# Turned activations with the channel chunk innermost, layer norms turned through HBM, and maxima gathered off TensorE

## The chip, the core and the metric

The program runs on one core of a Trainium2 chip. The metric is device time in microseconds. Three runs of the kernel before took 1811.73 (the median), 1814.87 and 1811.0 us. Everything is float32. The engines are TensorE (PE in the profile; PEld is its weight load), VectorE (DVE), ScalarE (ACT), GpSimd (POOL) and SyncE (SP), which issues all DMAs in one queue. SBUF is the working memory of 128 partitions, PSUM the memory that TensorE writes to.

## What is computed

Two layers on X of shape (2, 1024, 512). Each layer normalises its input and adds to it causal attention with 16 heads of 32 channels (with rotary embedding) and a gated feed-forward, both fed with the same normalised input:

```python
xn = _layernorm(x, axis=-1)
x = x + _L0_attn_ref(xn, Wq, Wk, Wv, Wo) + _L0_ffn_ref(xn, w_gate, w_up, w_down)
xn = _layernorm(x, axis=-1)
x = x + _L1_attn_ref(xn, Wq, Wk, Wv, Wo) + _L1_ffn_ref(xn, gate_w, up_w, down_w, gate_s, up_s, down_s)
# attention: softmax(mask(rope(xn Wq.T) @ rope(xn Wk.T).T * 32 ** -0.5)) @ (xn Wv.T), then @ Wo.T
# feed-forward: (silu(xn gate.T) * (xn up.T)) @ down.T, hidden width 2048 in layer 0, 1408 in layer 1
```

## The kernel before

The work is four phases, one for each layer and batch entry: (layer 0, b 0), (0, 1), (1, 0), (1, 1). A phase has 1024 tokens in eight tiles x of 128, and the normalised input turned to channels by tokens in two halves xnT of 512 tokens. The 512 channels are four chunks of 128, so a half of xnT is a tile of 128 partitions by [4 chunks, 512 tokens], and one chunk's 512 tokens lie side by side in each partition.

Products of xnT go through a scheme with seven block products in place of eight (`Unit`, L710): one unit for each 128 hidden columns (`Hidden`, L1131: gate and up together), one for each group of four heads (`QueriesKeys`, L901), two for the values (`Values`, L951). A unit has four pieces. `first` multiplies with the first half of xnT, `second` with the differences xs, `third` with the second half, `fourth` with the last difference again. Every block product is two matmuls (`product`, L760), with the weights as the stationary operand and xnT or xs as the moving one, 512 columns; in `Values.product` (L992) it is the other way round, xnT or xs being loaded as the weights, 128 columns at a time. GpSimd makes xs from xnT (`ln_sums`, L680) and at last writes differences over the first two chunks of xnT's second half (`ln_last_sum`, L691).

Attention of a phase goes over four groups of four heads and, in each, four blocks of 256 queries, a `Run` (L1207): 64 runs of one to four steps, 160 steps in all. A step makes scores (sc), which ScalarE copies to SBUF with the factor (s). VectorE takes maxima of s over blocks of 32 keys and 32 queries (rmax), and at the end of a run over the keys (m1, `blocks`, L1259). `maxima` (L1278) then gathers the partitions' parts: TensorE turns m1 into a PSUM tile (mtr), VectorE reduces it to m2, SP writes m2 to HBM (md), and `spread` (L1288) reads it back to all 128 partitions (mb). `transpose_maxima` (L1199) holds a finished run until its m1 is there by the planner's times. VectorE then subtracts mb, ScalarE takes exponentials, GpSimd adds them up (acc), and four steps later TensorE multiplies them with the values (av).

Layer norm of the first phase is done at the start, in pairs of tiles (`ln_pair`, `transpose_pair`, L633). For later phases, tiles are loaded and their statistics taken some 22 steps before the phase ends (`load_raw`, `ln_stats`, `ln_factors`). At the end of the phase they are loaded a second time (xr), scaled by ScalarE in place (`ln_scale`, L661), turned by four TensorE transposes into a bank of PSUM (`ln_transpose`, L668, the tile tr) and copied to xnT by ScalarE. A phase's input was written to HBM a phase earlier, or is the program's.

Order comes from a planner. `Schedule` (L155) records every operation with an estimated cost and places it in time, so that nearly all operations have line 278 in the profile; `again` (L358) makes the final order for every engine from due times reckoned backwards from TensorE's. `queue_phase` (L1552) lists the work that fills the gaps of attention, and `Fill.choose` (L1503) picks from it. The tiles tr, mtr, ux, uy, uz, d and ps_o share three banks of PSUM. The pool `tmp` holds two tiles for each tag, among them "swapped" (also used for the rotary embedding) and "xs" (also xr); `xp`, with xnT, has one for each tag.

Of the kernel before, what the change touches and what calls it, by code (L numbers as in the profile page):

```python
# [18 lines left out]
P = 128  # L19
# [11 lines left out]
NSQ = QB // SQ  # L31
EPS = 1e-5
# [122 lines left out]
class Schedule:  # L155
# [31 lines left out]
    def cost(self, eng, method, args, kwargs, outs, ins):  # L187

        n = self.columns(outs[0]) if outs else 0
        if eng is self.sync:  # L190

            size = 4 * int(np.prod((outs or ins)[0].shape, dtype=int))
            return 450.0, 1900.0 + size / self.RATE
        if eng is self.tensor:
            if method == "transpose":
                mode, t = "full", 131.0
            else:
                lhs, rhs = args[1], args[2]
                small_k, small_m = lhs.shape[0] < P, lhs.shape[1] < P
                mode = "rows" if small_k else "columns" if small_m else "full"  # L200
                t = max(self.columns(rhs), 64) * 1.676 / (1 if mode == "full" else 4)
            if mode != self.mode:
                t += {"full": 218.0, "columns": 100.0, "rows": 200.0}[mode]
                self.mode = mode
            return t, t + 163.0
        m = max([n] + [self.columns(i) for i in ins])
        if eng is self.vector:
            if method == "stream_shuffle":
                t = 735.0
            elif method == "reciprocal":  # L210
                t = 204.0
            elif method == "tensor_reduce" and not kwargs.get("apply_transpose"):
                t = (150.0 if ins[0].tile.pool.psum else 110.0) + m * (0.93 if ins[0].tile.pool.psum else 1.85)
            elif method == "bn_aggr":
                t = 182.0
            else:
                t = 160.0 + m * 1.04
        elif eng is self.scalar:
            t = (190.0 if method == "activation" and args[2] in self.TABLES else 150.0) + 0.85 * n
            for k in ("bias", "scale"):  # L220
                t += 105.0 if isinstance(kwargs.get(k), View) else 0.0
            t += 140.0 if method == "mul" else 0.0
        elif method == "affine_select":
# [282 lines left out]
def two_layers(ctx: ExitStack, tc: tile.TileContext, x_in, attn_w, ffn_w, ffn_s, rope, out):  # L506
# [126 lines left out]
    def transpose_pair(pair):  # L633

        tb, h = divmod(pair, 2)
        if h == 0:
            xnT[0, tb] = xp.tile([P, DC, TB], F32, tag=f"xnT{tb}", name=f"xnT0_{tb}")
        xn = normed.pop((0, pair))
        for n in range(2):
            tr = p_st.tile([P, 2, DC, P], F32, tag="st", name=f"tr0_{2 * pair + n}")  # L640
            for c in range(DC):
                nc.tensor.transpose(tr[:, 0, c, :], xn[:, n, ts(c, P)], ident)
            (nc.vector.tensor_copy if n else nc.scalar.copy)(xnT[0, tb][:, :, ts(2 * h + n, P)], tr[:, 0])
        if tb == 1:
            for n in range(2):
                ln_sums(0, 2 * h + n)
# [14 lines left out]
    def ln_scale(ph, t):  # L661
        tb, q = divmod(t, 4)
# [3 lines left out]
        normed[ph, t] = s  # L666

    def ln_transpose(ph, t):  # L668
        tb, q = divmod(t, 4)
        if q == 0:  # L670
            xnT[ph, tb] = xp.tile([P, DC, TB], F32, tag=f"xnT{tb}", name=f"xnT{ph}_{tb}")
        s = normed.pop((ph, t))
        tr = bank(f"tr{ph}_{t}", (P, DC, P))
        for c in range(DC):
            nc.tensor.transpose(tr[:, c, :], s[:, ts(c, P)], ident)
        nc.scalar.copy(xnT[ph, tb][:, :, ts(q, P)], tr)
        if tb == 1:
            ln_sums(ph, q)

    def ln_sums(ph, q):  # L680

        if q == 0:
            xs[ph] = [xp.tile([P, 2, TB], F32, tag=f"xs{n}", name=f"xs{n}_{ph}") for n in (1, 2, 4)]
        t1, t2, t4 = (t[:, :, ts(q, P)] for t in xs[ph])
        b11, b21 = (xnT[ph, 0][:, 2 * c : 2 * c + 2, ts(q, P)] for c in range(2))
        b12, b22 = (xnT[ph, 1][:, 2 * c : 2 * c + 2, ts(q, P)] for c in range(2))
# [4 lines left out]
    def ln_last_sum(ph):  # L691

        for c in range(2):
            b12, b22 = xnT[ph, 1][:, c, :], xnT[ph, 1][:, 2 + c, :]
# [15 lines left out]
    class Unit:  # L710
# [49 lines left out]
        def product(self, bank, a, b, start=False):  # L760
            for c in range(2):
# [3 lines left out]
                    b[:, c, :],  # L765
# [14 lines left out]
        def needs(self, kind):  # L780

            if kind == "second":
# [7 lines left out]
        def first(self):  # L790
# [4 lines left out]
            self.product(self.x, a11, x0[:, 0:2], start=True)  # L795
            one = self.one = keep(self.x, f"p1{self.name}")
            z = bank(f"uz{self.name}")
            self.product(z, a12, x0[:, 2:4], start=True)
# [18 lines left out]
        def third(self, nxt):  # L817
            (_, _, s3, _), _, s4 = self.blocks()
            x1 = xnT[self.ph, 1]
            self.product(self.x, s3, x1[:, 0:2])  # L820
# [3 lines left out]
            self.product(self.y, s4, x1[:, 2:4])  # L824
# [59 lines left out]
    def project_qk(which, tokens):  # L884
# [4 lines left out]
        for c in range(DC):  # L889
            nc.tensor.matmul(  # L890
                ps, wqk[0, 0, which][:, c, :], xnT[0, half][:, c, at : at + n], start=(c == 0), stop=(c == DC - 1)
# [59 lines left out]
    class Values(Unit):  # L951
# [154 lines left out]
    def hidden(ph, k, tb):  # L1106
# [3 lines left out]
        def product(name):  # L1110
            ps[name] = bank(f"{name}{ph}_{k}_{tb}")
            for c in range(DC):
                nc.tensor.matmul(
                    ps[name], wgu[ph, k, name][:, c, :], xnT[ph, tb][:, c, :], start=(c == 0), stop=(c == DC - 1)
# [80 lines left out]
    found = []  # L1195

    def transpose_maxima(now=False):
        while found and (now or nc.settled(found[0].m1) <= nc.tensor.free):
            found.pop(0).maxima()  # L1199
            spread_maxima()  # L1200

# [5 lines left out]
    class Run:  # L1207
# [208 lines left out]
    class Fill:  # L1416
# [111 lines left out]
        def run(self, step, share, between=()):  # L1528

            spent = 0.0  # L1530
            while True:
# [5 lines left out]
                transpose_maxima()  # L1537
# [14 lines left out]
    def queue_phase(ph):  # L1552
# [48 lines left out]
        def raw(t):  # L1601
            if t < QC:
                load_raw(nxt, t)

        def scale(t):
            if t < QC:
                ln_scale(nxt, t)


        fill.main.insert(len(fill.main) - 2, (0.0, lambda: (raw(0), raw(1)), "other", None, 0))  # L1610
        fill.main.insert(len(fill.main) - 1, (0.0, lambda: scale(0), "other", None, 0))
        for t in range(QC):

            def one(t=t):
                ln_transpose(nxt, t)
                raw(t + 2)
                scale(t + 1)

            fill.add(0.7, one, "other", lambda t=t: [normed[nxt, t]])
            if t == 1:  # L1620
                fill.add(0.0, waits)
        fill.add(0.0, lambda: (ln_last_sum(nxt), marks.append(nxt)))
# [56 lines left out]
    for i in range(total + LAG):  # L1679
# [52 lines left out]
        transpose_maxima(True)  # L1732
        if run and n == run.steps - 1:
            found.append(run)
# [78 lines left out]
```

## Time and profile before

| | |
|---|---|
| runs | 1811.73 us median (1811.0 to 1814.87) |
| the profiled execution's own time | 1814.8 us |
| its span in the profile | 1812.9 us |
| granted clock of TensorE | 0.998 |
| instructions in the span | 25807 |
| DMA | 165.15 MB, mean 91 GB/s |
| chain that ended last | PE 89%, POOL 5%, DVE 3%, issue 1%, ACT 1%, DMA 1% |

The page gives each engine's busy time, a picture of the span in 40 slices, the chain of work that ended last, groups of instructions and DMAs. A group's line reads: line, engine, operation, out<-in by the program's names, shapes, count | busy us in total, mean ns of one | idle time before them, and what ended it. A line of waits gives engine, tile and line, whom it waited for, us in total, times, the longest. A line of the timeline gives the start, the length, the engine, the operation and how many were merged. Matmuls overlap and their ends are modelled, so the distance between two starts says more than a mean length does. Names that stand for several tiles are merged: m is both m1 and m2, ws the weight sums, s the scores.

### The profile page before, as it was taken

The numbers are of one execution on the slowest core, as the hardware profiler recorded it, in microseconds if no ns is written. First come the engines' busy times: TensorE is split into PE (matmuls) and PEld (weight loads), VectorE is DVE, ScalarE is ACT, GpSimd is POOL, SyncE is SP. The second block draws the span as 40 slices with busy tenths as digits, with TensorE's granted clock in tenths as the row PEclk, the third lists the DMA queues.
The fourth block names the chain that finished last, engine by engine and source line by source line (L and its number), as shares of the span: only waits on it lengthen the run. The fifth ranks groups of instructions, "written<-read, shape, count | busy, mean of one in ns | idle before, by whom it ended". The sixth has DMA issues, their size and how long they took to land.

```text
span 1812.9 us, 25807 instructions
## 1 busy us (share of the span) xinstructions
PE 1798.0 (99%) x9406; PEld 880.0 (49%) x9406; DVE 1476.3 (81%) x1975; ACT 1041.7 (57%) x1240; POOL 1232.6 (68%) x1145
## 2 busy tenths in 40 slices
PE   9999999999999999999999999999999999999998
PEld 5464444444444644444444455444444464444443
DVE  3665988868879668779697798888979998989988
ACT  2444665556546565554575556576565757565762
POOL 6726875956868337446377894886779775866775
PEclk9999999999999999999999999999999999999999
DMA  5324343222232422222133324222223322221211
GB/s 192 99 82 137 114 148 120 67 80 82 80 113 88 138 72 68 70 82 89 56 97 102 115 76 160 76 80 71 77 84 98 125 69 71 70 69 50 67 39 71
DMA packets 140334, 165.15 MB, mean 91 GB/s; under 512 B 13360, under 2 KB 93488, under 8 KB 140208
## 3 DMA queue, kind: packets, MB, share of 16 engines
q1 hardware_dynamic: 140208, 163.50, 28.5%
q8 instruction: 75, 1.23, 0.3%
q14 instruction: 51, 0.42, 0.1%
HBM read 134.62 MB, written 28.84 MB: 90 GB/s over the span
## 4 chain that ended last, share of the span: by engine, by line
PE 89%; POOL 5%; DVE 3%; issue 1%; ACT 1%; DMA 1%; SPq 0%; POOLq 0%; ACTq 0%; DVEq 0%
PE d L278 24%; PE ux L278 19%; PE uy L278 9%; PE sc L278 8%; PE av L278 7%; PE ux_qk L278 5%; PE uz L278 5%; POOL acc L278 2%; PE uy_qk L278 2%; PE ux_v L278 2%; PE uz_qk L278 1%; PE uy_v L278 1%; DVE s L278 1%; PE ps_o L278 1%; PE tr L278 1%
## 5 line engine op out<-in xcount | busy, mean ns | idle before, releaser
L278 POOL TENSOR_TENSOR acc<-acc,s 128x512 f32<-128x512 f32 (+1 forms) x378 | 487.4, 1311 | 84.4 <-ACT s L278 79.9
L278 DVE TENSOR_TENSOR s<-s,mb 128x512 f32<-128x512 f32 (+1 forms) x384 | 489.6, 1300 | 12.5 <-DMA mb<-md 12.5
L278 DVE TRANSPOSE_TENSOR_REDUCE rmax<-s 128x32 f32<-128x1024 f32 (+1 forms) x320 | 351.5, 1117 | 63.9 <-POOL s L278 41.3
L278 PE MATMUL d<-wd,hT 128*128 128x512 f32 x864 | 400.1, 593 | 0.0
L278 ACT ACTIVATE s<-s 128x1024 f32<-128x1024 f32 (+1 forms) x320 | 304.9, 970 | 163.0 <-DVE s L278 161.0
L278 ACT ACTIVATE s<-sc 128x1024 f32<-128x1024 f32 (+1 forms) x320 | 283.3, 934 | 195.1 <-PE sc L278 184.0
L278 POOL TENSOR_TENSOR acc<-s 128x512 f32<-128x512 f32 (+1 forms) x128 | 169.2, 1328 | 195.3 <-ACT s L278 191.5
L278 PEld LDWEIGHTS d<-wd,hT 128*128 128x128 f32 x864 | 161.9, 190 | 192.6 <-issue 186.9
L278 ACT ACT_TABLE_LOAD x167 | 214.3, 1283 | 7.7 <-DVE s L278 4.7
L278 DVE TENSOR_TENSOR x<-d,x 128x512 f32<-128x512 f32 x224 | 151.3, 676 | 75.8 <-PE d L278 75.0
L278 PE MATMUL av<-s,v 128*32 128x256 f32 (+1 forms) x2560 | 159.2, 364 | 0.7 <-ACT s L278 0.5
L278 POOL TENSOR_SCALAR_AFFINE_SELECT s<-s 128x512 f32<-128x512 f32 x128 | 98.9, 784 | 67.0 <-ACT s L278 65.0
L278 PEld LDWEIGHTS av<-s,v 128*32 128x32 f32 x2560 | 67.6, 109 | 145.7 <-issue 97.2
L278 POOL TENSOR_TENSOR hT<-p,hT 128x512 f32<-128x512 f32 x53 | 72.5, 1367 | 77.9 <-ACT hT L278 77.9
L278 PE MATMUL d<-wo,oT 128*128 128x512 f32 x198 | 103.0, 602 | 1.2 <-DVE hT L278 1.2
L278 PE MATMUL ux<-xs,ws 128*128 128x512 f32 x212 | 101.7, 602 | 0.6 <-ACT p L278 0.6
L278 PE MATMUL ux<-xnT,wu 128*128 128x512 f32 x212 | 101.8, 602 | 0.1
L278 PE MATMUL ux<-xnT,wg 128*128 128x512 f32 x212 | 100.9, 598 | 0.4 <-DVE hT L278 0.4
L278 PE MATMUL ux<-xs,wu 128*128 128x512 f32 x212 | 101.2, 600 | 0.0
L278 PE MATMUL uy<-xs,ws 128*128 128x512 f32 x212 | 99.7, 593 | 0.3 <-DVE hT L278 0.3
L278 PE MATMUL uy<-xnT,ws 128*128 128x512 f32 x212 | 99.8, 593 | 0.0
L278 PE MATMUL uz<-xnT,wg 128*128 128x512 f32 x212 | 99.7, 593 | 0.0
(179 smaller groups left out, 2511.2 us busy)
## 6 DMA issues: line engine op xcount, KB each, us to landing
mb<-md SPq DMA_DIRECT2D x64, 512.0 KB, 3.8
wg<-in_gate SPq DMA_DIRECT2D x54, 256.0 KB, 2.9
wd<-in_down SPq DMA_DIRECT2D x32, 256.0 KB, 2.9
xr<-xm SPq DMA_DIRECT2D x32, 256.0 KB, 2.7
wu<-in_up SPq DMA_DIRECT2D x28, 256.0 KB, 3.0
s12gu<-ws SPq DMA_DIRECT2D x26, 256.0 KB, 2.0
ws<-s12gu SPq DMA_DIRECT2D x26, 256.0 KB, 2.6
wd<-wds SPq DMA_DIRECT2D x22, 256.0 KB, 2.9
```

The source lines that it names most:

```text
L278: target(*[get(a) for a in args], **{k: get(a) for k, a in kwargs.items()})
```

## The change

Four things change.

1. **The layout of xnT and xs.** xnT becomes [128, 512 tokens, 4 chunks] and xs [128, 512 tokens, 2], chunk innermost. All readers index the chunk last, so that a matmul's 512 columns are four floats apart in xnT, and two apart in xs.
2. **Layer norms of phases 1 to 3.** After `ln_scale` VectorE turns each tile in squares of 32 by 32, writing with the chunk innermost. Four DMAs, one for each 32 tokens, write it to HBM so that a channel's row holds 32 tokens by 4 chunks (512 bytes) from each; `ln_read` later reads a tile of 128 channels by 2 KB back into xnT. The transposes and copies of `ln_transpose` are gone. Loading, statistics, scaling and turning all run in steps 24 to 11 before the phase's end; the reads stand at the phase's last unit, the first half before its `second`, the second half before its `fourth`. The xs sums of all four quarters follow in one go after that unit.
3. **Maxima.** In `maxima`, VectorE turns m1 in squares of 32, ScalarE copies four blocks of 32 partitions side by side, and VectorE reduces these. It is called at the end of the run's last step instead of through `transpose_maxima`.
4. **The planner** sees xnT's first half as a need of `first`, and sizes a stationary operand by all its columns.

```diff
     def ln_scale(ph, t):
...
         nc.scalar.activation(s, s, AF.Identity, bias=off[:, q : q + 1], scale=rstd[:, q : q + 1])
-        normed[ph, t] = s
+        turned_x = tmp.tile([P, QSQ, SQ, DC], F32, tag="swapped", name=f"xt{ph}_{t}")
+        nc.vector.transpose(turned_x.rearrange("p f s c -> p c f s"), s.rearrange("p (c f s) -> p c f s", f=QSQ, s=SQ))
+        to = normed[ph, t] = xd.tile([P, QSQ, P], F32, tag=f"xn{t}", name=f"xnd{ph}_{t}")
+        for a in range(QSQ):
+            nc.sync.dma_start(
+                out=to[:, a, :].rearrange("(f s) e -> s f e", s=SQ),
+                in_=turned_x[ts(a, SQ)].rearrange("p f s c -> p f (s c)"),
+            )
+
+    def ln_read(ph, tb):
+        xnT[ph, tb] = xp.tile([P, TB, DC], F32, tag=f"xnT{tb}", name=f"xnT{ph}_{tb}")
+        for q in range(4):
+            nc.sync.dma_start(
+                out=xnT[ph, tb][:, ts(q, P)].rearrange("p t c -> p (t c)"), in_=normed.pop((ph, 4 * tb + q)).rearrange("p a e -> p (a e)")
+            )
...
-        tr = bank(f"tr{ph}_{t}", (P, DC, P))
-        for c in range(DC):
-            nc.tensor.transpose(tr[:, c, :], s[:, ts(c, P)], ident)
-        nc.scalar.copy(xnT[ph, tb][:, :, ts(q, P)], tr)
...
-            xs[ph] = [xp.tile([P, 2, TB], F32, tag=f"xs{n}", name=f"xs{n}_{ph}") for n in (1, 2, 4)]
+            xs[ph] = [xp.tile([P, TB, 2], F32, tag=f"xs{n}", name=f"xs{n}_{ph}") for n in (1, 2, 4)]
...
                 nc.tensor.matmul(
                     bank,
                     a[:, c, :],
-                    b[:, c, :],
+                    b[:, :, c],
...
-                        b[:, c, ts(2 * self.pair + n, P)],
+                        b[:, ts(2 * self.pair + n, P), c],
                         a[:, c, :],
...
         def maxima(self):
 
-            tr = bank(f"mtr{self.name}", (HG * NSQ, P))
-            nc.tensor.transpose(tr, self.m1.rearrange("p h b -> p (h b)"), ident)
+
+            mt = small.tile([P, SQ], F32, tag="mt", name=f"mt_{self.name}")
+            nc.vector.transpose(mt, self.m1.rearrange("p h b -> p (h b)"))
+            mg = small.tile([HG * NSQ, P // SQ, SQ], F32, tag="mg", name=f"mg_{self.name}")
+            for a in range(P // SQ):
+                nc.scalar.copy(mg[:, a, :], mt[ts(a, SQ), :])
             m2 = small.tile([HG * NSQ, SQ], F32, tag="m2", name=f"m2_{self.name}")
-            nc.vector.tensor_reduce(m2, tr.rearrange("c (a p) -> c p a", p=SQ), AX.X, ALU.max)
+            nc.vector.tensor_reduce(m2, mg.rearrange("c a s -> c s a"), AX.X, ALU.max)
...
             for t in range(QC):
-                fill.at(t0 + per_phase - 22 + t, lambda t=t: load_raw(nxt, t))
-                fill.at(t0 + per_phase - 21 + t, lambda t=t: ln_stats(nxt, t))
-            fill.at(t0 + per_phase - 12, lambda: ln_factors(nxt, range(2)))
+                fill.at(t0 + per_phase - 24 + t // 2, lambda t=t: load_raw(nxt, t))
+                fill.at(t0 + per_phase - 23 + t // 2, lambda t=t: ln_stats(nxt, t))
+            fill.at(t0 + per_phase - 19, lambda: ln_factors(nxt, range(2)))
+            for t in range(QC):
+                fill.at(t0 + per_phase - 19 + t, lambda t=t: load_raw(nxt, t))
+                fill.at(t0 + per_phase - 18 + t, lambda t=t: ln_scale(nxt, t))
...
+        fill.main.insert(len(fill.main) - 3, (0.0, lambda: ln_read(nxt, 0), "other", None, 0))
+        fill.main.insert(len(fill.main) - 1, (0.0, lambda: ln_read(nxt, 1), "other", None, 0))
+        fill.add(0.0, waits)
+
+        def sums():
+            for q in range(4):
+                ln_sums(nxt, q)
+            ln_last_sum(nxt)
+            marks.append(nxt)
+
+        fill.add(0.0, sums)
```

More of the change, by code (lines that the diff above doesn't have):

```diff
@@ L31 @@
 NSQ = QB // SQ
+QSQ = P // SQ
 EPS = 1e-5
@@ L198, in cost @@
                 lhs, rhs = args[1], args[2]
-                small_k, small_m = lhs.shape[0] < P, lhs.shape[1] < P
+                small_k, small_m = lhs.shape[0] < P, self.columns(lhs) < P
                 mode = "rows" if small_k else "columns" if small_m else "full"
@@ L636, in transpose_pair @@
         if h == 0:
-            xnT[0, tb] = xp.tile([P, DC, TB], F32, tag=f"xnT{tb}", name=f"xnT0_{tb}")
+            xnT[0, tb] = xp.tile([P, TB, DC], F32, tag=f"xnT{tb}", name=f"xnT0_{tb}")
         xn = normed.pop((0, pair))
@@ L642, in transpose_pair @@
                 nc.tensor.transpose(tr[:, 0, c, :], xn[:, n, ts(c, P)], ident)
-            (nc.vector.tensor_copy if n else nc.scalar.copy)(xnT[0, tb][:, :, ts(2 * h + n, P)], tr[:, 0])
+            (nc.vector.tensor_copy if n else nc.scalar.copy)(
+                xnT[0, tb][:, ts(2 * h + n, P)], tr[:, 0].rearrange("p c t -> p t c")
+            )
         if tb == 1:
@@ L665, in ln_scale @@
         nc.scalar.activation(s, s, AF.Identity, bias=off[:, q : q + 1], scale=rstd[:, q : q + 1])
-        normed[ph, t] = s
[L668 to L672, printed above, removed]
-        tr = bank(f"tr{ph}_{t}", (P, DC, P))
-        for c in range(DC):
-            nc.tensor.transpose(tr[:, c, :], s[:, ts(c, P)], ident)
-        nc.scalar.copy(xnT[ph, tb][:, :, ts(q, P)], tr)
-        if tb == 1:
-            ln_sums(ph, q)
+        turned_x = tmp.tile([P, QSQ, SQ, DC], F32, tag="swapped", name=f"xt{ph}_{t}")
[11 more added lines that the diff above has]
+                out=xnT[ph, tb][:, ts(q, P)].rearrange("p t c -> p (t c)"), in_=normed.pop((ph, 4 * tb + q)).rearrange("p a e -> p (a e)")
+            )
     def ln_sums(ph, q):
         if q == 0:
-            xs[ph] = [xp.tile([P, 2, TB], F32, tag=f"xs{n}", name=f"xs{n}_{ph}") for n in (1, 2, 4)]
-        t1, t2, t4 = (t[:, :, ts(q, P)] for t in xs[ph])
-        b11, b21 = (xnT[ph, 0][:, 2 * c : 2 * c + 2, ts(q, P)] for c in range(2))
-        b12, b22 = (xnT[ph, 1][:, 2 * c : 2 * c + 2, ts(q, P)] for c in range(2))
+            xs[ph] = [xp.tile([P, TB, 2], F32, tag=f"xs{n}", name=f"xs{n}_{ph}") for n in (1, 2, 4)]
+        t1, t2, t4 = (t[:, ts(q, P)] for t in xs[ph])
+        b11, b21 = (xnT[ph, 0][:, ts(q, P), 2 * c : 2 * c + 2] for c in range(2))
+        b12, b22 = (xnT[ph, 1][:, ts(q, P), 2 * c : 2 * c + 2] for c in range(2))
         nc.gpsimd.tensor_tensor(t1, b12, b11, ALU.subtract)
@@ L693, in ln_last_sum @@
         for c in range(2):
-            b12, b22 = xnT[ph, 1][:, c, :], xnT[ph, 1][:, 2 + c, :]
+            b12, b22 = xnT[ph, 1][:, :, c], xnT[ph, 1][:, :, 2 + c]
             nc.gpsimd.tensor_tensor(b12, b22, b12, ALU.subtract)
@@ L780, in needs @@
         def needs(self, kind):
+            if kind == "first":
+                return [xnT[self.ph, 0]]
             if kind == "second":
@@ L794, in first @@
             self.x = bank(f"ux{self.name}", hold=True)
-            self.product(self.x, a11, x0[:, 0:2], start=True)
+            self.product(self.x, a11, x0[:, :, 0:2], start=True)
             one = self.one = keep(self.x, f"p1{self.name}")
             z = bank(f"uz{self.name}")
-            self.product(z, a12, x0[:, 2:4], start=True)
+            self.product(z, a12, x0[:, :, 2:4], start=True)
             self.c11(z, one)
@@ L819, in third @@
             x1 = xnT[self.ph, 1]
-            self.product(self.x, s3, x1[:, 0:2])
+            self.product(self.x, s3, x1[:, :, 0:2])
             if nxt:
@@ L823, in third @@
             self.c22(self.x, self.p5)
-            self.product(self.y, s4, x1[:, 2:4])
+            self.product(self.y, s4, x1[:, :, 2:4])
             let_go(f"uy{self.name}")
@@ L890, in project_qk @@
             nc.tensor.matmul(
-                ps, wqk[0, 0, which][:, c, :], xnT[0, half][:, c, at : at + n], start=(c == 0), stop=(c == DC - 1)
+                ps, wqk[0, 0, which][:, c, :], xnT[0, half][:, at : at + n, c], start=(c == 0), stop=(c == DC - 1)
             )
@@ L1113, in product @@
                 nc.tensor.matmul(
-                    ps[name], wgu[ph, k, name][:, c, :], xnT[ph, tb][:, c, :], start=(c == 0), stop=(c == DC - 1)
+                    ps[name], wgu[ph, k, name][:, c, :], xnT[ph, tb][:, :, c], start=(c == 0), stop=(c == DC - 1)
                 )
@@ L1193, in two_layers @@
     waiting, rows = [], [0]
[L1195 to L1200, printed above, removed]
     def spread_maxima():
@@ L1536, in run @@
                     continue
-                transpose_maxima()
                 chosen = self.choose(step)
@@ L1598, in queue_phase @@
             return
[L1601 to L1622, printed above, removed]
+        fill.main.insert(len(fill.main) - 3, (0.0, lambda: ln_read(nxt, 0), "other", None, 0))
[7 more added lines that the diff above has]
+        fill.add(0.0, sums)
         fill.add_unit(QueriesKeys(nxt, 0, 0), slices[0])
@@ L1731, in two_layers @@
             between.pop(0)()
-        transpose_maxima(True)
         if run and n == run.steps - 1:
-            found.append(run)
+            run.maxima()
+            spread_maxima()
         carried = goal - spent
```

## The prediction

> **What bounds the kernel now.** I read the page's first two parts first, to see which engine has no time left and at what clock.
>
> ```profile
> PE 1798.0 (99%) x9406; PEld 880.0 (49%) x9406; DVE 1476.3 (81%) x1975; ACT 1041.7 (57%) x1240; POOL 1232.6 (68%) x1145
> PEclk9999999999999999999999999999999999999999
> ```
>
> TensorE (PE) is busy 99% at full clock; every other engine has over 300 us spare. The waits of PE then show whether that figure hides stalls.
>
> ```profile
> PE av L278 <- DVE sums L278: 3.1, 7, 1.1
> PE tr L278 <- ACT xn L278: 2.0, 1, 2.0
> ```
>
> These are the longest waits of all, so no wait is worth removing: the time is the sum of PE's instructions, and the change is worth what it does to that sum. A busy time is no price, because matmuls overlap; the timeline gives the price as the distance between starts.
>
> ```profile
> 462.81 1.04 PE L278 MATMUL tr<-ident,xr 128*128 128x128 f32 x8
> 463.76 1.12 PE L278 MATMUL d<-wo,oT 128*128 128x512 f32 x2
> 614.42 1.88 PE L278 MATMUL ux<-xnT,wg 128*128 128x512 f32 x4
> 616.14 0.59 PE L278 MATMUL uz<-xnT,wg 128*128 128x512 f32 x1
> ```
>
> Four products of 512 columns take 616.14 - 614.42 = 1.72 us: 0.43 us each, 0.84 ns a column, though the groups give their mean as 0.60. Eight transposes of 128 columns take 463.76 - 462.81 = 0.95 us: 0.12 us each.
>
> Last, PE's groups with shapes kept apart say who reads the turned activations xnT. The trace counts two instructions for each float32 matmul of the code.
>
> ```profile
> L278 PE MATMUL ux<-xnT,wu 128*128 128x512 f32 x212 | 101.8, 602 | 0.1
> L278 PE MATMUL ux<-xnT,wg 128*128 128x512 f32 x212 | 100.9, 598 | 0.4 <-DVE hT L278 0.4
> L278 PE MATMUL uy<-xnT,ws 128*128 128x512 f32 x212 | 99.8, 593 | 0.0
> L278 PE MATMUL uz<-xnT,wg 128*128 128x512 f32 x212 | 99.7, 593 | 0.0
> L278 PE MATMUL ux_qk<-xnT,wk 128*128 128x512 f32 x60 | 28.8, 603 | 0.0
> L278 PE MATMUL mtr<-ident,m 128*32 128x128 f32 x64 | 18.0, 281 | 0.1
> L278 PE MATMUL tr<-ident,xr 128*128 128x128 f32 x96 | 14.5, 277 | 0.0
> ```
>
> **What it removes from PE.** 96 transposes tr at 0.12 us are 11.4 us. 64 transposes of maxima mtr: from its start to the next matmul's the trace has 0.13 us (610.85 to 610.98), so 8 to 9 us. Together -20 us, all on the path. Two users of the three shared PSUM banks go too, worth nothing where PE never waits for a bank.
>
> **What it changes without naming it.** xnT is turned inside out, from [128, 4, 512] to [128, 512, 4]. A matmul that took 512 neighbouring floats now takes every fourth, a step of 16 bytes. These are four groups of 212 (848), four of 60 in the queries and keys (ux_qk with wq and wk, uz_qk, uy_qk: 240), and in the start 32 for g and u, 16 of 512 and 32 of 256 columns for ps_k and ps_q: 1152 instructions of 512 columns, 1152 x 0.429 = 494 us of PE, over a quarter of the run. No matmul of before reads with such a step, so the price must be bounded. The nearest rows are VectorE's reductions of rmax, which step through SBUF by 64 bytes or more, and its reduction of mtr, which steps through PSUM:
>
> ```profile
> L278 DVE TENSOR_REDUCE m<-rmax 128x32 f32<-128x256 f32 x16 | 9.3, 580 | 0.3
> L278 DVE TENSOR_REDUCE m<-rmax 128x32 f32<-128x192 f32 x16 | 7.5, 470 | 0.2
> L278 DVE TENSOR_REDUCE m<-rmax 128x32 f32<-128x128 f32 x16 | 5.8, 360 | 0.3
> L278 DVE TRANSPOSE_TENSOR_REDUCE rmax<-s 128x32 f32<-128x1024 f32 x192 | 232.8, 1224 | 22.4 <-ACT s L278 21.8
> L278 DVE TRANSPOSE_TENSOR_REDUCE rmax<-s 128x24 f32<-128x768 f32 x128 | 118.7, 955 | 41.5 <-POOL s L278 41.3
> L278 DVE TENSOR_REDUCE m<-mtr 32x32 f32<-32x128 f32 x64 | 17.2, 269 | 18.6 <-PE mtr L278 17.9
> ```
>
> Stepping through SBUF costs (580 - 360) / 128 = 1.72 ns an element, twice the same; neighbours cost (1224 - 955) / 256 = 1.05. The mtr row, 269 ns for 128 from PSUM, has no room for 1.72 x 128 = 220 beside its fixed part, so the penalty belongs to SBUF and not to the reduction. 1.72 ns is no whole number of the 1.05 ns steps, which looks like the memory's own time for a fresh line rather than VectorE's. PE asks for a float every 0.84 ns, in transposes too (0.12 us for 128), so no row shows slack on its reading side. At 1.72 ns an instruction takes 512 x 1.72 = 0.88 us instead of 0.43.
>
> [...]Bounds: 0, if PE takes each float in two halves and so hits the line twice; +315 us, if only VectorE's ratio 1.72 / 1.05 carries over; +494 for a doubling; +520 at 1.72 ns. A gain is excluded, since no row is under 0.84 ns. I take the doubling, 1.68 ns a column, 2% from the row.
>
> **Smaller items.** The xs sums become pairs of neighbours (8-byte steps, two hits a line): at 1.72 / 2 = 0.86 ns against 0.84, 816 instructions by 11 ns are at most 9 us; I take 0. The 256 products of the values load xnT as weights, 128 columns each, now stepped: 128 x 1.72 = 220 ns against a spacing of 216 to hide in. I take +5 us, between 0 and 256 x 0.16 = 41 (today's 0.19 us load doubled to 0.38, less 0.22 hidden).
>
> Off PE, nothing is charged, with its cover. ScalarE gets four small copies a run, 256 by about 0.19 us (the rows of 512 and 256 columns, 585 and 372 ns, give 0.83 ns a column and 0.16 fixed): 48 us, less 24 evictions by 0.58: +34 on 57% busy. VectorE gets 24 turns of 512 elements near the shuffle's 0.735 us, doubled at worst by the stepped writes (18 to 35 us), and 64 of 32 columns at about 0.2 us (13 us): up to +50 on 81%. GpSimd does the same twelve sums and two last ones a phase, stepped: 13 us, perhaps 18. SP issues 96 writes and 24 reads at 0.3 to 0.45 us, some 45 us over 1813. On its queue a write that waits for its turn on VectorE holds up the maxima (md, mb) and weight loads behind it; the weight loads have a spare buffer, the maxima are the third rival. All moved loads and scales of the next layer norm need inputs a phase old, so nothing new is waited for there. At each of three transitions the reads of xnT's second half wait for the last product that reads the old one; four transfers (about 5 us at 2.7 landing) and the sums (13) follow, 18 us, against PE work of 1.7 (fourth), 13.7 (16 down products by 0.86), 3.4 (first) and some 4 of attention: 23 us. It is covered, else 5 us each, 15 in all.
>
> **The sum**, against the profiled execution's 1814.8 us (span 1812.9 and 1.9 around it; the runs' median 1811.7 lies 3 below): -20 + 494 + 5 = +479, so 2294, and 2291 on the runs' footing. I say 2290.
>
> **Rivals.**
> First, stepped reads are free for PE. [...]Against: the 1.72 ns row and transposes at the same pace. Then -20 with 0 to 15 of stalls at transitions and loads: 1792 to 1807, likeliest 1796. This is the other side: faster. It decides from 20 / 1152 = 17 ns an instruction: a penalty under 4% still leaves a gain.
>
> Second, the penalty is VectorE's ratio: 1812 + 315 - 20 = 2107.
>
> Third, reads free, but the maxima come later: a turn of 0.2 us, four copies behind ScalarE's queue (an activation of 1 us and a table load of 1.3 may stand ahead) and the DMAs in SP's order, for one transpose. VectorE already waits 12.5 us for mb. If 1 to 2 us per run reach PE in the 16 longest, that is +16 to +32: 1808 to 1824.
>
> **How the numbers follow.** A measurement tells 0.2% from no change, 1808 to 1815. Doubling or near it 0.47, the ratio case 0.10 (both slower); reads free with the gain 0.29; free and eaten up 0.06; free and slower by late maxima or transitions 0.08. So faster 0.29, same 0.06, slower 0.65. The likeliest case's own range is 2100 to 2340 (520, weights 41 and the ratio case as ends); both signs hold much chance, so the range runs from 1788 to 2335.
>
> **What would show it.** Right: the distance between starts of ux<-xnT,wu near 0.86 us while ux<-xs and d stay at 0.43; tr (but for the first phase's) and mtr gone; PE still near 99%, the other shares fallen. Wrong: those distances at 0.43, and the time near 1796. The third rival would show as PE waiting for s or sums behind DMA mb. An intermediate distance means the memory hides part of a line's time.

## The result, and the profile after

The changed kernel takes 2358.2 us (median of four runs, 2356.01 to 2358.89) where the kernel before, on the same chip, takes 1812.74 (1811.0 to 1814.87): a ratio of 1.301, 95% interval 1.299 to 1.303, or 545 us more. The profiled execution took 2358.55 us with a span of 2356.7, so 543.8 more span than before's 1812.9. The granted clock is 0.998 in both. The forecast was 2290 with a range up to 2335: the sign and the mechanism came, the size was 68 us short and lay outside the range.

First the page's busy shares, its clock row, and its chain by engine:

```profile
PE 2344.4 (99%) x9246; PEld 898.6 (38%) x9246; DVE 1452.6 (62%) x2062; ACT 1081.0 (46%) x1468; POOL 1193.5 (51%) x1148
PEclk9999999999999999999999999999999999999999
...
PE 98%; DVE 1%; ACT 0%; DMA 0%; issue 0%; SPq 0%; DVEq 0%
```

TensorE has 160 instructions fewer (the 96 transposes and 64 maxima) and 546 us more to do; the other engines' busy times moved by 40 us or less, so their shares fell. The longest waits of TensorE are even smaller than before's:

```profile
PE av L279 <- DVE sums L279: 2.3, 3, 1.0
PE av L279 <- DVE oT L279: 1.7, 2, 1.4
```

So nothing new holds TensorE up: its own instructions became longer. The timeline of the changed kernel says which.

```profile
613.95 1.88 PE L279 MATMUL d<-wd,hT 128*128 128x512 f32 x4
617.83 3.84 PE L279 MATMUL ux<-xnT,wu 128*128 128x512 f32 x4
621.50 1.08 PE L279 MATMUL uy<-xnT,ws 128*128 128x512 f32 x1
```

Four products of xnT now take 621.50 - 617.83 = 3.67 us, with about 0.1 us of a restart in it; over the whole trace the distance between two starts is 0.900 us where it was 0.429. The groups with shapes kept apart tell the same about all users:

```profile
L279 PE MATMUL d<-wd,hT 128*128 128x512 f32 x864 | 401.4, 596 | 0.0
L279 PE MATMUL ux<-xnT,wu 128*128 128x512 f32 x212 | 201.8, 1086 | 0.0
L279 PE MATMUL uy<-xnT,ws 128*128 128x512 f32 x212 | 200.3, 1079 | 0.0
L279 PE MATMUL ux<-xs,wu 128*128 128x512 f32 x212 | 106.9, 625 | 0.0
L279 PE MATMUL uz_v<-wv,xnT 128*128 128x256 f32 x64 | 16.2, 397 | 0.0
```

d, whose operands the change leaves alone, is where it was (596 ns in the mean, 593 before). A group of xnT costs 100 us more than before (201.8 against 101.8). xs, two floats apart, costs about 5% more than d (625 against 596). The values, which load xnT as weights, are hardly touched (397 against 381).

With each start distance sorted, TensorE's span comes apart as follows, in us. "Products" are full 512-column matmuls at their plain distance (429, 450 or 900 ns); a "restart" is 60 to 150 ns on top of one, a "hole" is more; the rest is small tiles (scores, av, values, transposes, and the start's products of 256 columns).

| | products | restarts | holes | rest |
|---|---|---|---|---|
| before | 1317.5 | 27.2 (277) | 1.7 (4) | 460.0 |
| after | 1869.7 | 30.1 (320) | 3.8 (9) | 447.1 |
| layout alone | 1869.7 | 26.1 (273) | 0 | 463.2 |
| maxima alone | 1317.5 | 31.8 (322) | 12.1 (21) | 453.1 |
| after, xnT in blocks | 1317.5 | 32.6 (330) | 10.1 (17) | 451.3 |
| the same, maxima on TensorE | 1317.5 | 28.8 (294) | 6.4 (11) | 446.3 |

After less before, the products are 552.2 more: 1136 instructions on xnT by 0.471 = 535.1, and 816 on xs by 0.021 = 17.1. Everything else together takes 8 back.

### The profile page after: what moved, and what is told of

Same layout as the page of the kernel before. It is cut to its first block, busy times and chain, and to the rows that moved or that the text cites. A ratio compares the mean times of both kernels' runs of the same rounds, so it can differ in the third digit from the quotient of the medians.

```text
span 2356.7 us, 25999 instructions
## 1 busy us (share of the span) xinstructions
PE 2344.4 (99%) x9246; PEld 898.6 (38%) x9246; DVE 1452.6 (62%) x2062; ACT 1081.0 (46%) x1468; POOL 1193.5 (51%) x1148
## 4 chain that ended last, share of the span: by engine, by line
PE 98%; DVE 1%; ACT 0%; DMA 0%; issue 0%; SPq 0%; DVEq 0%
PE ux L279 25%; PE d L279 19%; PE uy L279 12%; PE uz L279 8%; PE ux_qk L279 7%; PE sc L279 7%; PE av L279 6%; PE uy_qk L279 3%; PE ux_v L279 2%; PE uz_qk L279 2%; PE ps_o L279 1%; PE uy_v L279 1%; PE uz_v L279 1%; PE ps_k L279 1%; PE ps_q L279 1%; PE g L279 1%
## 5 line engine op out<-in xcount | busy, mean ns | idle before, releaser
L279 POOL TENSOR_TENSOR acc<-acc,s 128x512 f32<-128x512 f32 x382 | 470.7, 1253 | 165.7 <-ACT s L279 156.8
L279 DVE TENSOR_TENSOR s<-s,mb 128x512 f32<-128x512 f32 (+1 forms) x384 | 429.8, 1145 | 9.4 <-DMA mb<-md 9.4
L279 POOL TENSOR_TENSOR acc<-s 128x512 f32<-128x512 f32 (+1 forms) x127 | 161.6, 1279 | 250.0 <-ACT s L279 249.2
L279 ACT ACT_TABLE_LOAD x163 | 209.1, 1283 | 16.5 <-DVE s L279 13.6
L279 PE MATMUL ux<-xnT,wu 128*128 128x512 f32 x212 | 201.8, 1086 | 0.0
L279 PE MATMUL uz<-xnT,wg 128*128 128x512 f32 x212 | 200.3, 1079 | 0.0
L279 PE MATMUL uy<-xnT,ws 128*128 128x512 f32 x212 | 200.3, 1079 | 0.0
L279 PE MATMUL ux<-xnT,wg 128*128 128x512 f32 x212 | 200.2, 1078 | 0.0
L279 DVE TENSOR_TENSOR hT<-uz,p 128x512 f32<-128x512 f32 x53 | 36.6, 691 | 189.1 <-PE uz L279 189.1
L279 POOL TENSOR_SCALAR_AFFINE_SELECT s<-s 128x512 f32<-128x512 f32 x128 | 89.5, 713 | 83.2 <-ACT s L279 81.5
L279 ACT ACTIVATE hT<-hT 128x512 f32<-128x512 f32 x62 | 39.1, 630 | 192.5 <-DVE hT L279 192.4
```

Of the source, the lines that this page charges most:

```text
L279: target(*[get(a) for a in args], **{k: get(a) for k, a in kwargs.items()})
```

## The experiments

My theory was that the layout alone makes the time: TensorE pays for every fresh line of 16 bytes. The rivals were that transfers and late maxima have a large share, and that the step is dear for another reason than the line.

**What a step costs (e5).** A kernel of its own, with no part of the computation, streams 512 columns at steps of 1, 2, 3, 4, 5, 6, 8 and 16 floats. The rest of its code does the same in bf16 (b_), with stepped weights (w_), and on VectorE (r_) and ScalarE (a_):

```diff
+    for k, word in WORDS.items():
+        run("f_" + word, big[:, 0 : 512 * k].rearrange("p (n k) -> p n k", k=k)[:, :, 0], w)
+    run("f_pairs", big[:, 0:1024].rearrange("p (n k) -> p n k", k=4)[:, :, 0:2], w)
+    run("f_fours", big[:, 0:1024].rearrange("p (n k) -> p n k", k=8)[:, :, 0:4], w)
+    run("f_shifted", big[:, 0:1024].rearrange("p (n k) -> p n k", k=8)[:, :, 2:6], w)
...
```

> No part of the computation: repeated matmuls of 512 columns, 16 to each kind, whose moving operand steps by 1, 2, 3, 4, 5, 6, 8 and 16 floats (f_), pairs of neighbours every 16 bytes, fours on and off a 16-byte line every 32 bytes, the same steps in bf16 (b_), weights with steps (w_), and VectorE maxima and ScalarE copies of 512 elements with steps. Theory (a fresh 16-byte line costs TensorE 1.76 ns, a float at least 0.84): steps of 1 and of 2 floats 429 and 450 ns an instruction, 3 floats 0.75 of 900 = 675, 4 and all above 900; pairs at 16 bytes 450, fours on a line 429, fours off a line 450. VectorE and ScalarE: 1.7 ns an element from a step of 4 on. Rival (the cost grows with the distance, or is TensorE's alone): 16 floats dearer than 4, or ScalarE at its 0.83 ns with any step.

Its groups; each name is one pattern. Busy us divided by the count comes close to the distance between starts:

```profile
L38 PE MATMUL f_one<-big 128*128 128x512 f32 x32 | 13.9, 592 | 0.0
L38 PE MATMUL f_two<-big 128*128 128x512 f32 x32 | 14.6, 611 | 0.0
L38 PE MATMUL f_three<-big 128*128 128x512 f32 x32 | 21.8, 847 | 0.0
L38 PE MATMUL f_four<-big 128*128 128x512 f32 x32 | 29.0, 1078 | 0.0
L38 PE MATMUL f_sixteen<-big 128*128 128x512 f32 x32 | 27.6, 1034 | 0.0
L38 PE MATMUL f_fours<-big 128*128 128x512 f32 x32 | 13.9, 592 | 0.0
L38 PE MATMUL f_shifted<-big 128*128 128x512 f32 x32 | 14.6, 611 | 0.0
L38 PE MATMUL b_four<-half 128*128 128x512 bf16 x16 | 7.4, 629 | 0.0
...
L56 DVE TENSOR_REDUCE r_one<-big 128x1 f32<-128x512 f32 x4 | 2.7, 686 | 14.3 <-DMA big<-in_x 14.2
L56 DVE TENSOR_REDUCE r_three<-big 128x1 f32<-128x512 f32 x4 | 3.4, 846 | 0.1
L56 DVE TENSOR_REDUCE r_four<-big 128x1 f32<-128x512 f32 x4 | 4.3, 1081 | 0.1
L57 ACT COPY a_one<-big 128x512 f32<-128x512 f32 x4 | 2.5, 617 | 0.1
L57 ACT COPY a_three<-big 128x512 f32<-128x512 f32 x4 | 3.5, 885 | 0.1
L57 ACT COPY a_four<-big 128x512 f32<-128x512 f32 x4 | 4.5, 1131 | 0.1
```

The starts stand 429 ns apart for steps of one float, 450 for two, 676 for three, 900 for four, and 858 to 918 for every longer one. Counted in lines of 16 bytes, each column has one of its own at four floats: 900 / 512 = 1.76 ns a line. A step of three touches 384 lines, 384 x 1.76 = 675; a step of two 256, 450. It is the count of lines and not the step itself: four floats side by side, then a gap of four, cost 429 if they fill a line (f_fours) and 450 if they lie across two (f_shifted, 256 lines). Nor does the type matter: in bf16, 512 neighbours take 216 ns, every second 226 (128 lines), every fourth 451 (256), every eighth 900 (512). All of these fit one count: an instruction takes the longer of its columns' time (429 ns in fp32, 216 in bf16) and some 1.76 ns by its lines. The 1.76 is not exact, since steps of over four floats, also with a line for each column, lie between 1.68 (858 / 512) and 1.79 (918 / 512), and why they differ is open. VectorE (686 to 1081) and ScalarE (617 to 1131) slow down at the same steps; from three floats to four, 128 lines more, they pay (1081 - 846) / 128 = 1.84 and (1131 - 885) / 128 = 1.92 ns a line.

The price of a line is not TensorE's own pace, for it stays when TensorE's clock halves. The bf16 matmuls with a step of 16 bytes happen to run into such a stretch at 290.3 us. A row of stretches gives start and end, the length, each engine's busy time (PE, PEld, DVE, ACT, POOL), and then the granted clock, here 0.50:

```profile
290.30:299.80 9.50, 9.50 (x11) 1.28 (x10) 0.00 (x0) 0.00 (x0) 0.00 (x0) 0.50 0.01 2
```

They start every 900 ns before it and within it, while the short matmuls with neighbouring weights behind them start every 213 ns at half clock and every 111 at full. Weights stepped by 16 bytes let the next matmul of 128 columns start after 233 ns, where weights two floats apart take 118 and neighbours 111.

**The layout alone (e1).** Before, with xnT and xs inside out; transposes and maxima stay on TensorE.

```diff
-            xnT[ph, tb] = xp.tile([P, DC, TB], F32, tag=f"xnT{tb}", name=f"xnT{ph}_{tb}")
+            xnT[ph, tb] = xp.tile([P, TB, DC], F32, tag=f"xnT{tb}", name=f"xnT{ph}_{tb}")
...
-        nc.scalar.copy(xnT[ph, tb][:, :, ts(q, P)], tr)
+        nc.scalar.copy(xnT[ph, tb][:, ts(q, P)], tr.rearrange("p c t -> p t c"))
...
-                    b[:, c, :],
+                    b[:, :, c],
```

> The kernel before with the changed layout of xnT and xs alone; transposes and maxima stay on TensorE. Theory (all of the loss is TensorE's stepped reads): 1152 instructions by 471 ns (900 instead of 429) are 543 us, 816 on xs by 21 ns are 17, 256 weight loads of the values by 17 ns are 4; 1812.7 + 564 = 2377 us, some 20 above the changed kernel. Rival (late maxima or the layer norms through HBM carry a part): below 2358 us by that part.

2366.8 us, 1.307 times before (1.304 to 1.309), +555. Page and group:

```profile
PE 2355.0 (100%) x9406; PEld 909.1 (38%) x9406; DVE 1433.8 (61%) x1975; ACT 1046.4 (44%) x1240; POOL 1198.9 (51%) x1145
...
L278 PE MATMUL ux<-xnT,wu 128*128 128x512 f32 x212 | 201.0, 1082 | 0.0
```

Before's 9406 instructions on TensorE, after's price in the group. The layout makes the whole loss; the other edits together are worth 2366.8 - 2358.2 = 9 us (10 when each run is set against before on its own chip), about half of the 20 forecast.

**After, with xnT in blocks (e3).** If the step is the cause, another layout must give it back while the transfers, the turns and the maxima stay. Each 128 tokens now lie as [chunk, token], so that a matmul reads four runs of 128 neighbours. Each tile is read back in four DMAs instead of one.

```diff
-        xnT[ph, tb] = xp.tile([P, TB, DC], F32, tag=f"xnT{tb}", name=f"xnT{ph}_{tb}")
+        xnT[ph, tb] = xp.tile([P, 4, DC, P], F32, tag=f"xnT{tb}", name=f"xnT{ph}_{tb}")
...
-        turned_x = tmp.tile([P, QSQ, SQ, DC], F32, tag="swapped", name=f"xt{ph}_{t}")
+        turned_x = tmp.tile([P, QSQ, DC, SQ], F32, tag="swapped", name=f"xt{ph}_{t}")
...
-            xs[ph] = [xp.tile([P, TB, 2], F32, tag=f"xs{n}", name=f"xs{n}_{ph}") for n in (1, 2, 4)]
+            xs[ph] = [xp.tile([P, 4, 2, P], F32, tag=f"xs{n}", name=f"xs{n}_{ph}") for n in (1, 2, 4)]
```

> The changed kernel with xnT as four blocks of 128 tokens, in each the four chunks with 128 neighbouring tokens; the turned tiles keep their 512-byte writes to HBM, the reads come in pieces of 128 bytes (16 instead of 4 DMAs for each half). Maxima and layer norms as in the changed kernel. Theory: all 564 us of stepped reads go, the 20 us of transposes stay away: 1793 us, up to 1808 with stalls at the transitions. Rival (the moved layer norms or maxima cost by themselves): above 1813 us.

1821.5 us, 1.005 times before (1.0038 to 1.0062). Its group of ux, VectorE's turn in it, and TensorE's longest waits:

```profile
L279 PE MATMUL ux<-xnT,wu 128*128 128x512 f32 x212 | 102.4, 605 | 0.0
...
L279 DVE STREAM_TRANSPOSE xt<-xr 128x512 f32<-128x512 f32 x24 | 16.6, 691 | 2.8 <-ACT xr L279 2.4 <-POOL k_3T L279 0.4
```

```profile
PE av L279 <- DVE sums L279: 6.4, 8, 2.0
PE av L279 <- ACT s L279: 5.5, 4, 2.2
```

ux is back at 102 us and 537 us are gone from the run (2358.2 - 1821.5): the theory holds. But the run is not the 1792 to 1807 that cheap reads should leave; TensorE waits for attention somewhat longer than before (6.4 us for sums where it was 3.1).

**The maxima alone (e2).** Before, with only edit 3; the layer norms stay on TensorE.

```diff
-            tr = bank(f"mtr{self.name}", (HG * NSQ, P))
-            nc.tensor.transpose(tr, self.m1.rearrange("p h b -> p (h b)"), ident)
+            mt = small.tile([P, SQ], F32, tag="mt", name=f"mt_{self.name}")
+            nc.vector.transpose(mt, self.m1.rearrange("p h b -> p (h b)"))
+            mg = small.tile([HG * NSQ, P // SQ, SQ], F32, tag="mg", name=f"mg_{self.name}")
+            for a in range(P // SQ):
+                nc.scalar.copy(mg[:, a, :], mt[ts(a, SQ), :])
...
-            found.append(run)
+            run.maxima()
+            spread_maxima()
```

> The kernel before with the maxima gathered by VectorE and ScalarE, nothing else changed. Theory: 64 transposes by 0.13 us leave TensorE, 1804 us. Rival (the maxima come later and the wait reaches TensorE in the 16 longest runs): 1820 to 1836 us.

1821.2 us, 1.0053 (1.004 to 1.0066): +10 where -8 was forecast. Waits of TensorE, VectorE and ScalarE (us, times, the longest), and the chain just before the end of the run:

```profile
PE av L278 <- ACT s L278: 4.9, 3, 2.2
PE av L278 <- DVE sums L278: 4.3, 5, 2.0
...
ACT mg L278 <- DVE mt L278: 56.0, 36, 4.9
...
DVE m L278 <- ACT mg L278: 29.5, 37, 2.3
```

```profile
1794.75 0.22 DVE mt L278
1795.00 0.22 ACT mg L278
1795.23 0.22 ACT mg L278
...
1795.68 0.22 ACT mg L278
1795.93 0.37 DVE m L278
```

ScalarE stands 56 us for VectorE's turn, and VectorE 30 us for ScalarE's copies. Near the end the two hand each other the maxima on the path itself, 1.5 us for what the prediction charged at nothing. TensorE's timeline there, and rows of stretches with the granted clock (0.50, 1.00, 0.50), show a second cost:

```profile
1778.48 1.06 PE L278 MATMUL av<-s,v 128*32 128x256 f32 x12 [1.75 <-ACT s L278]
1779.46 5.40 PE L278 MATMUL d<-wd,hT 128*128 128x512 f32 x8
1784.79 0.86 PE L278 MATMUL av<-s,v 128*32 128x256 f32 x16
```

```profile
1779.70:1783.10 3.40, 3.40 (x5) 1.34 (x5) 2.38 (x4) 1.69 (x2) 3.40 (x3) 0.50 0.43 147
1783.10:1800.20 17.10, 14.07 (x84) 5.87 (x83) 13.15 (x22) 4.67 (x8) 11.87 (x12) 1.00 0.12 38
1800.20:1807.00 6.80, 5.62 (x11) 2.50 (x12) 4.28 (x8) 1.58 (x2) 2.33 (x5) 0.50 0.20 63
```

After a wait of 1.75 us, eight products take 1784.79 - 1779.46 = 5.33 us instead of 8 x 0.43 = 3.4, because TensorE runs at half clock for 3.4 us of it, and from 1800 for another 6.8. Before has no such stretch between its first 20 us and TensorE's last instruction. The next ten runs ask what makes the 10 us.

**Only the end? (e6, e7)** The last group's four runs keep their maxima on TensorE, in e2 (e6) and in e3 (e7).

```diff
+            self.on_tensor = (ph, g) == (len(phases) - 1, NG - 1)
...
+            if self.on_tensor:
+                tr = bank(f"mtr{self.name}", (HG * NSQ, P))
+                nc.tensor.transpose(tr, self.m1.rearrange("p h b -> p (h b)"), ident)
```

> e2_maxima_only with the maxima of the last group of heads (four runs) back on TensorE. Theory (late maxima cost only at the end, where TensorE has little else to do: of the 16.6 us that e2_maxima_only adds in holes of over 0.6 us between TensorE's starts, 11.2 lie after 1700 us): 60 transposes saved are 8 us, 5 us of holes stay, 1811.5 - 8 + 5 = 1808 to 1811 us. Rival (ScalarE's copies hold up its queue in the whole run): 1817 to 1821 us.

> e3_in_blocks with the maxima of the last group back on TensorE. Theory (the end alone): 1821.5 - 10 = 1811 us or less, down to 1801 if the holes near 1400 us go too. Rival (the whole run): 1817 us or more. Against e4_blocks_pe_maxima (1805.7) it tells if maxima off TensorE gain anything where TensorE has other work: below 1805.7 they do.

1817.7 us (1.003, 1.002 to 1.004) and 1815.1 (1.0017, 1.001 to 1.0023): e6 lies where the rival had it, e7 between the two. The end accounts for some 4 us of e2 and 7 of e3, not for all. In the profiled execution of e6 the stretches at half clock are gone; those of e3 fall from 13.6 us to 6.8 in e7.

**The copies? (e10, e11)** e10 makes each copy twice; e11 makes none and takes the maxima of the first 32 partitions only.

```diff
# e10
             for a in range(P // SQ):
-                nc.scalar.copy(mg[:, a, :], mt[ts(a, SQ), :])
+                for _ in range(2):
+                    nc.scalar.copy(mg[:, a, :], mt[ts(a, SQ), :])
# e11
-            for a in range(P // SQ):
-                nc.scalar.copy(mg[:, a, :], mt[ts(a, SQ), :])
...
-            nc.vector.tensor_reduce(m2, mg.rearrange("c a s -> c s a"), AX.X, ALU.max)
+            nc.vector.tensor_reduce(m2, mt[ts(0, SQ), :].rearrange("c (s a) -> c s a", a=1), AX.X, ALU.max)
```

> e2_maxima_only with each of ScalarE's four copies made twice: 256 more by 0.215 us, 55 us of ScalarE and 0.9 us more to each run's chain of maxima. Theory (the chain through ScalarE is what costs, by its length): about 10 us more than e2_maxima_only, 1828 to 1834 us. Rival (the copies are free, VectorE's turn or the changed order costs): 1819 to 1823 us.

> e2_maxima_only without the copies: the maxima are taken from the first 32 partitions of the turned tile alone, so three quarters of the blocks are left out of them, and ScalarE has no part in the chain. Theory (ScalarE's part is the cost): 1802 to 1808 us, the 8 us of transposes saved. Rival (VectorE's turn and the changed order cost by themselves): 1814 us or more.

Twice the copies: 1844.8 us (1.0182, 1.0168 to 1.0196), 24 us over e2. None: 1821.3 (1.0056, 1.0043 to 1.007), just e2's time. More copies cost, but without the ones that are there the run is no faster, so they alone don't make the 10 us. Neither of my expectations of e10 had it so dear.

**ScalarE's queue? (e8, e9)** The copies go to VectorE, in e3 (e8) and in e2 (e9).

```diff
-                nc.scalar.copy(mg[:, a, :], mt[ts(a, SQ), :])
+                nc.vector.tensor_copy(mg[:, a, :], mt[ts(a, SQ), :])
```

> e3_in_blocks with the four copies of the gathered maxima on VectorE instead of ScalarE, so that the chain stays on one engine. Theory (what counts is that the maxima come later at the end, on whichever engine): four copies by about 0.2 us remain, the waits between the engines go; 1815 to 1821 us. Rival (ScalarE's queue standing behind VectorE is the cost): 1803 to 1808 us.

> e2_maxima_only with the four copies on VectorE. Theory (later maxima at the end): 1814 to 1821 us. Rival (ScalarE's queue): 1803 to 1807 us.

1876.7 us (1.0355, 1.0341 to 1.0369) and 1864.9 (1.0291, 1.0277 to 1.0305), far above every expectation. The group of these copies in e9:

```profile
L278 DVE COPY mg<-mt 32x32 f32<-32x32 f32 x256 | 100.9, 394 | 4.9
```

The mean is 394 ns and the longest 1366, about as long as one of GpSimd's additions (1.3 us). The 138 copies during which GpSimd runs nothing take 174 ns at most, the 118 that overlap one of its instructions 656 in the mean: the long ones come where GpSimd works at the same time. VectorE is then busy 85% and the path gets 44 us longer. So putting the copies on ScalarE was the better choice, and ScalarE's queue isn't what costs the 10 us.

**The time of the call? (e12, e13)** The maxima are held back again by `transpose_maxima` as before, in e2 (e12) and in e3 (e13).

```diff
+                transpose_maxima()
...
+        transpose_maxima(True)
...
-            run.maxima()
-            spread_maxima()
+            found.append(run)
```

> The kernel before with the maxima by VectorE and ScalarE as in e2_maxima_only, but held back as before until the planner's times say that m1 is there, instead of being called at the end of the run's last step. Theory (the earlier call reorders what is recorded after it, and that costs the 18 us between e2_maxima_only and the expected 1804): 1802 to 1810 us. Rival (TensorE loses as much in restarts and holes wherever the chain is called, since its work no longer has the gap-filling transposes and VectorE's queue is fuller): 1818 us or more.

> e3_in_blocks with the maxima held back in the same way. Theory (the time of the call): 1792 to 1803 us, below e4_blocks_pe_maxima (1805.7). Rival: 1815 us or more.

1825.8 us (1.0078, 1.0066 to 1.0091) and 1829.7 (1.0106, 1.009 to 1.0121): slower still. The earlier call of the change helps by 5 to 8 us.

**VectorE's load? (e14, e15)** Both leave out the factor of the sines in the rotary embedding, 64 products on VectorE; e14 is before, e15 is e2.

```diff
-        nc.vector.tensor_tensor(swapped, swapped, sin[:, cols], ALU.mult)
```

> The kernel before without the 64 products with the sines in the rotary embedding (left out: that factor), which were 67 us of VectorE's 1476. It is the partner of e15_maxima_light_vector. TensorE's work is unchanged and it is the bound: 1806 to 1812 us under both theories.

> e2_maxima_only without the same 64 products. Theory (the chain of maxima costs because VectorE, which carries it and is 82 to 93% busy in the second half, has no slack there to hide it): with 67 us less on VectorE the transposes' 8 us show, or at least the loss of 10 us goes: 8 to 0 us under e14_before_light_vector. Rival (TensorE's restarts and holes come with the changed order, whatever VectorE's load): 8 us or more above it.

1811.3 us (0.9995, 0.9987 to 1.0003) and 1825.9 (1.007, 1.0056 to 1.0084). With a lighter VectorE the maxima cost 14.6 us, not less. This theory falls too.

**In blocks, with the maxima on TensorE (e4).** What is left is the transfers' part alone: layer norms turned ahead of time, neighbours read, maxima as before.

```diff
# against e3
-            for a in range(P // SQ):
-                nc.scalar.copy(mg[:, a, :], mt[ts(a, SQ), :])
+            tr = bank(f"mtr{self.name}", (HG * NSQ, P))
+            nc.tensor.transpose(tr, self.m1.rearrange("p h b -> p (h b)"), ident)
```

> As e3_in_blocks, with the maxima back on TensorE as in the kernel before. Theory: only the 96 transposes of layer norm are saved, 1812.7 - 11.4 = 1801 us, 8 above e3_in_blocks. Rival (late maxima cost more than 8 us): below e3_in_blocks.

1805.7 us against 1811.5 before (0.9978, 0.9969 to 0.9988; 22 runs): the only version that beats both kernels, though by a mere 0.2%. In spans it is 1805.4 against 1812.9. Without the 96 transposes (11.4 us by the forecast) the "rest" of the table falls by 13.7; restarts (+1.6) and holes (+4.7) take 6.3 of it back.

## Why the prediction was right in its mechanism and wrong in its size

**The bound.** Right: TensorE's sum decides. In e1 the other engines' work is before's, and the whole edit shows in the time.

**The step of 16 bytes, +494.** Right in kind, too small. The prediction chose a doubling, 1.68 ns a column, because it came within 2% of VectorE's row of 1.72. The upper bound that it named beside it (+520) was nearer: the measured 1.76 ns, against today's 0.84, gives 1136 x 0.471 = 535 and, for the 32 instructions of 256 columns, 7.5: 543. This term is 49 us short, and it is the step that failed. VectorE's row had shown nearly the right time for a line all along, from an engine of another pace; there was no reason to round it down to twice TensorE's own pace. That TensorE could take each float in two halves and so pay nothing, the bound of 0, was the author's conjecture: no run shows it, and in e5 a step of four floats takes 900 ns, 2.1 times the 429 of neighbours.

**xs, taken as 0, at most 9.** It was 17.1: 816 x 21 ns. The term supposed two floats to a line, which no run had shown by then; e5 has 450 ns for 512 columns in steps of two, as for 256 lines. At 1.76 / 2 = 0.88 ns a float the line sets the time, above the 0.84 of neighbours. The bound of 9 came from VectorE's 1.72 / 2, a little under TensorE's 1.76 / 2, and then the term was put at nothing.

**The values' weights, +5 (0 to 41).** Right: the distance went from 216 to 233 ns, 256 x 17 ns = 4.4. The load of uz_v itself went from 190 to 329 ns, and 17 of these 139 show.

**The removal, -20.** It came to -9 (after less e1), for two reasons. The first is the 64 mtr, priced at 8 to 9 by the distance from a mtr's start to the next matmul's. These lines of before's timeline show what that overlooked:

```profile
609.78 1.15 PE L278 MATMUL sc<-q_1T,k_0T 32*128 32x256 f32 x16
610.85 0.28 PE L278 MATMUL mtr<-ident,m 128*32 128x128 f32 x1
610.98 1.02 PE L278 MATMUL ps_o<-wo,oT 128*128 128x512 f32 x2
611.84 0.81 PE L278 MATMUL ux_v<-wv,xs 128*128 128x256 f32 x3
...
622.38 1.15 PE L278 MATMUL sc<-q_1T,k_0T 32*128 32x256 f32 x16
623.46 1.98 PE L278 MATMUL ux<-xnT,wu 128*128 128x512 f32 x4
625.28 0.59 PE L278 MATMUL uy<-xnT,ws 128*128 128x512 f32 x1
```

Straight after scores four full products take 625.28 - 623.46 = 1.82 us, 0.10 more than 4 x 0.43: the first one after the small tiles pays a restart. With a mtr between, two take 611.84 - 610.98 = 0.86, no restart. Over the trace, from the last score to the second full product it is 837 ns (median) without a mtr and 858 with one: a mtr costs 21 ns there, and 109 only between full products. 39 of the 64 stand right after scores, so all are worth by this estimate some 39 x 0.021 + 25 x 0.11 = 3.6 us. The restarts answer: of the 277 before, 99 fall on the first full product after scores (149 on the last one ahead of an av); of the 322 in e2 these are 136, one more for nearly each of those 39. The second reason is the holes, below.

**Everything off TensorE, charged at nothing.** Right in this kernel, where each product became so long that all else has room: after has 3.8 us of holes. With short products it doesn't hold (e3: 10.1). The copies took 215 ns (0.19 forecast), and at the transitions GpSimd's sums wait 1.5 us in all for the reads, TensorE not at all. VectorE's turn was put at 0.735, doubled at worst:

```profile
L279 DVE STREAM_TRANSPOSE xt<-xr 128x512 f32<-128x512 f32 x24 | 26.0, 1082 | 0.9 <-ACT xr L279 0.9
...
L279 DVE TENSOR_REDUCE m<-mg 32x32 f32<-32x128 f32 x64 | 22.9, 358 | 30.5 <-ACT mg L279 30.1
L279 ACT COPY mg<-mt 32x32 f32<-32x32 f32 x256 | 55.0, 215 | 42.8 <-DVE mt L279 40.4
```

1082 ns with writes 16 bytes apart, 691 in e3's runs of neighbours: 1.57 times, inside the bounds. The reduction to m2 bears out how the prediction read the mtr row: from SBUF it takes 358 ns, as the rmax row of 128 does (360), where from PSUM it took 269.

**The third rival, late maxima.** With the step taken away it is what happens, and in its size: 1808 to 1824 forecast, 1821.5 in e3. That the number fits is in part luck, for its place was wrong. It was put into the 16 longest runs, behind ScalarE's queue; but without the copies (e11) nothing comes back, and the end gives 4 to 7 us (e6, e7). What is shown: moving the maxima off TensorE costs 10 us in before and 16 in e3 (1821.5 - 1805.7), of which about 4 are restarts each time. In e2 10 more are holes of TensorE (12.1 against 1.7), against some 7 that the small tiles take less. 4.2 us of these holes come from products at half clock. The profiled executions have half clock, between the first 20 us and TensorE's last instruction, for 10.2 us in e2 and 13.6 in e3, and for no time in before, e4 and e6; at the granted 0.50 such a stretch costs at most half its length. It isn't the whole cause either, as e11's has none and still took 1819.2 us. Why the planner's order, which comes out anew with every edit, has the other waits is open. The copies, the engine that makes them, the time of the call and VectorE's load are each ruled out as its single cause.

**The sum.** What failed above all is the price of the step, +494 for a doubling where the runs show +543; two smaller terms were mis-sized with it, xs and the removal. 49 (line price) + 17 (xs) + 11 (removal worth 9, not 20) - 1 (weights) is 76 more than forecast; measured was 545 - 479 = 66. The 9 or so missing show in e1 too, where the longer instructions add up to 564 and 555 was measured: with the longer products restarts and holes are 2.8 us less, and TensorE's waits before av and tr fall from 5.6 us to 1.7; the remainder I didn't follow further. The range was also added up too low. With the ends that the prediction names, 520 for the step and 41 for the weights, the sum is 1812 - 20 + 520 + 41 = 2353, and 2362 with xs' 9, not 2340 or 2335: its own bounds, added up, contain the 2358.

## What to carry to other kernels

A change of layout is a change of every instruction that reads the tile: count its readers on the bound engine before the work it removes, and keep each 16-byte line's floats together in the innermost run of a streamed operand (512 columns took 429 ns in e5, and 900 with a line for each; in blocks, with the layer norms still going through HBM, e4 is no slower than before). When a row of another engine shows a memory's price, take the row itself and multiply it out, instead of fitting it to the nearest round ratio. And price an instruction on a full engine by the sequence with and without it: what stands at a change of tile shape may be nearly free, as a mtr after scores was (21 ns, where it cost 109 between full products).

## What the runs showed of the hardware

- A matmul's stream took about 1.76 ns for each fresh 16-byte line (1.68 to 1.79 over the steps tried), in both types: 512 columns of fp32 took 429 ns side by side and 858 to 918 at 16 bytes or more; of bf16 216, and 451 already at 8 bytes, with two values from each line. VectorE and ScalarE slowed down at the same steps: at four floats 1081 and 1131 ns for 512 elements against 686 and 617.
- That price did not change with TensorE's clock: 900 ns at full clock and at half, where matmuls of neighbours doubled (111 to 213).
- Runs of 16 bytes that lie across two lines took as long as steps of 8 bytes: 450 ns, against 429 in f_fours.
- The first full matmul after the narrow tiles of scores lost about 0.1 us; a transpose standing in between absorbed it and cost 21 ns, where it cost 109 between full ones.
- Copies of 32 by 32 on VectorE, from SBUF to SBUF, took at most 174 ns while GpSimd ran nothing and 656 in the mean, up to 1366, while it did; ScalarE's took 215 (219 at most in e2).
- In e2 a wait of TensorE of 1.75 us was followed by 3.4 us at half clock (granted 0.50), and the eight products behind it took 5.33 us instead of 3.4. So that wait cost 1.75 us, and 1.9 more behind it. One of 2.6 us in e11 was followed by no such stretch.
